# Where the attention scores stand in the instruction order of an audio-tower kernel

## The chip, the cores and the metric

The kernel runs on one core of one Trainium2 chip. The metric is device time in microseconds (us) of one execution. Three runs of the kernel before gave 1310.27, 1310.64 and 1313.44 us; the median is 1310.64. Everything is float32.

## The reference

For 64 sequences of 157 tokens with 512 features each, the reference does four things. `h` below is one sequence.

```python
frames = pad(x).reshape(64, 157, 512)
h = frames @ dct.T                                   # tokenizer
n = layernorm(h)
key = exp(1j * pi * tanh(n @ Wk + bk))               # 4 sets of 8 phases
qry = exp(1j * pi * tanh(n @ Wq + bq))
V = n @ Wv + bv
total = sum over sets and planes of weight * Re(cumsum(key * V) * conj(qry))
total = gate * total + (1 - gate) * pos_contrib      # gate = sigmoid(n @ Wg + bg)
h = h + n + total / norm @ Wo + bo
n = layernorm(h)
e = argmax(softmax(mean(n, axis=tokens) @ Wg_ffn + bg_ffn))   # one of 16 experts per sequence
h = h + gate_e * (n @ We[e] + be[e])
```

The cumulative sum over tokens is computed as a causally masked score matrix (key against query phases) times V. Each sequence picks one expert, whose 512x512 weights are gathered from memory.

## The kernel before, in words

The batch is cut into 16 groups `g` of four sequences (GB = 4). The 160 padded tokens are five blocks of 32 (Q = 32), so that one tile of 128 rows holds block `n` of all four sequences, 32 rows each. Block number 4 is called TAIL.

The program text writes each engine's order by hand: an instruction is issued on its engine where it stands in the text, and engines meet only at semaphores. For a middle group the order is: `project_and_values(g)`, `gate(g)`, `experts_and_embedding(g)`, `attention(g)`. The stages of three groups are interleaved. While group `g` computes gate and attention, the experts of group `g-1` run and the tokens of group `g+1` are embedded.

`gate(g)` computes the gate by seven block products (a fast matrix product scheme), in the order 1, 6, 2, 7, 5, 4, 3. Each product is four matmuls (`gate_product`, line 655), which the chip runs as eight passes. Products 2, 4 and 3 accumulate onto the PSUM bank of an earlier one (1, 7 and 5), after VectorE has read that bank. Between the products stand the five embeddings of group `g+1` (`embed`, lines 270 and 272; `embed_statistics`, in which ScalarE copies two pieces out of PSUM, lines 292 and 293, and VectorE reads the rest, lines 100 and 99, then takes mean and variance). Block 0 is embedded after product 6, block 1 after product 2, and blocks 2, 3 and TAIL after product 3. After product 5 stand `scores(g)` and `fold_twice(g+1, 1)`.

`scores(g)` computes the key-query products. For each of the five blocks and each of the four sequences it issues one matmul (line 681), 20 in all, with 128x32 weights; the output goes to the 32 rows of its sequence and uses columns 0 to 479 (NS = 480) of a 512-column bank. Then VectorE masks the result (line 682) and adds the position share (line 683) into `att`, which `read` in `attention(g)` uses.

`experts_and_embedding(g)` runs three of the five expert tiles of group `g-1`: TAIL, 0 and 1. An expert tile (`expert`, `expert_chunk`, line 945) is 16 matmuls of 128x32 weights and 512 columns, which the chip runs as 32 passes. Four of them, one per sequence, sit side by side in the array's columns. The stationary operand is `x2T`, the turned and normalised activations, moved by 16 small DMAs; the moving operand is `we`, the expert weights, one gathered megabyte per sequence (`fetch`, line 899, an indirect DMA on the GpSimd queue). Tiles 2 and 3 of the experts follow inside `attention(g)`.

PSUM is one pool of four buffers of two banks each (`psum`, and `bank` for its first bank). A request takes the next buffer, and its first write waits until the last reader of the buffer's former content is done.

Of the kernel before, what the change touches and what calls it, by code (L numbers as in the profile page):

```python
# [25 lines left out]
GB = 4  # L26
NG = B // GB
LP = 160
Q = P // GB
# [18 lines left out]
NS = sum(hi - lo for lo, hi in SEES)  # L48
# [5 lines left out]
def audio_tower(ctx: ExitStack, tc: tile.TileContext, a, out):  # L54
# [21 lines left out]
    nc = tc.nc  # L76
# [14 lines left out]
    def psum():  # L91

        return ps_mm.tile([P, 2, 512], F32, tag="mm", name="mm")

    def bank():
        return psum()[:, 0, :]

    S = [{} for _ in range(NG)]
# [10 lines left out]
    def load_half(g, m):  # L109

        if g < NG:
            if m == 0:
                S[g]["xT"] = p1.tile([P, C, 2 * HN], F32, tag="xT", name="xT", bufs=2)
            nc.sync.dma_start(out=half(S[g]["xT"], m), in_=a["frames"][g, m])

    def fold_once(g, m, engine=nc.gpsimd):

        if g < NG:
            ft = half(S[g]["xT"], m)
            even = p2.tile([P, 2, HN], F32, tag="even", name="even")  # L120
            add(even, ft[:, :2], ft[:, 2:])
            engine.tensor_tensor(ft[:, :2], ft[:, :2], ft[:, 2:], ALU.subtract)
            S[g]["even", m] = even

    def fold_twice(g, m):

        if g < NG:
            ft, even = half(S[g]["xT"], m), S[g].pop(("even", m))
            add(ft[:, 2], even[:, 0], even[:, 1])
            sub(ft[:, 3], even[:, 0], even[:, 1])  # L130
            for n in range(2):
                to, by = ft[:, n], ft[:, 1 - n]
                nc.vector.scalar_tensor_tensor(to, by, lift[:, n : n + 1], to, ALU.mult, ALU.add)
# [101 lines left out]
    def deviation(rstd, var):  # L235

        nc.gpsimd.tensor_scalar(rstd, var, EPS, None, ALU.add)  # L237
        nc.gpsimd.tensor_tensor(rstd, rstd, power[:, : rstd.shape[-1]], ALU.pow)

    def shifts(mean, rstd):  # L240

        shift = small.tile([P, NM], F32, tag="shift", name="shift")[:, : rstd.shape[-1]]
        nc.gpsimd.tensor_tensor(shift, mean, rstd, ALU.mult)
        nc.gpsimd.tensor_scalar(shift, shift, -1.0, None, ALU.mult)  # L244
        return shift
# [13 lines left out]
    def embed(g, n):  # L259

        s = S[g]
        if n == 0:
            s["res"] = {}
            s["res2"] = []
        h = psum()
        h, odd = h[:, 0, :], h[:, 1, :].rearrange("p (n j) -> p n j", n=2)
        by_r = h.rearrange("p (j r) -> p r j", r=4)
        ft = tile_of(s["xT"], n)
        for i in range(2):
            nc.tensor.matmul(by_r[:, 2 * i, :], ft[:, 2 + i], dct_e[:, i, :], start=True, stop=True)  # L270
        for i in range(2):
            nc.tensor.matmul(odd[:, i, : P + 1], ft[:, i], trig_o[:, i, :], start=True, stop=True)  # L272
        s["h", n] = h, odd
# [30 lines left out]
    def embed_deviations(g, of=range(NM), known=False):  # L304

        s = S[g]
        lo, hi = min(SLOT[n] for n in of), max(SLOT[n] for n in of) + 1
        rstd, mv = deviations[g % 2][:, lo:hi], s["mv"][:, lo:hi]
        if not known:
            deviation(rstd, mv[:, :, 1])  # L310
        shift = shifts(mv[:, :, 0], rstd)
        more = small.tile([P, NM], F32, tag="more", name="more", bufs=6)[:, : hi - lo]
        nc.gpsimd.tensor_scalar(more, rstd, 1.0, None, ALU.add)  # L313
        for n in of:
            k = slice(SLOT[n] - lo, SLOT[n] - lo + 1)
            s["rstd", n] = rstd[:, k]
            s["st", n] = shift[:, k], more[:, k]
# [194 lines left out]
    def add_bv(g, m, of=slice(0, D)):  # L512
        v = S[g]["v2", m][:, :, of]
        by = bv[:, of].unsqueeze(1).to_broadcast([P, 2, of.stop - of.start])
        nc.gpsimd.tensor_tensor(v, v, by, ALU.add)  # L515
# [131 lines left out]
    def gate_product(g, i):  # L647

        s = S[g]
        if i == 1:  # L650
            s["gT"] = p1.tile([P, C, 2 * HN], F32, tag="gT", name="gT")
        (ps, first), rhs, w = room(g, i), operand(g, i), fac_g[i]
        for o in range(2):
            for c in range(2):
                nc.tensor.matmul(  # L655
                    ps[:, o, :HN],
                    w[:, c, o * P : (o + 1) * P],
                    rhs[:, c],
                    start=(first and c == 0),
                    stop=(c == 1),  # L660
                    skip_group_check=not first,
                )
        part = halves(s["gT"])
        if i != 2:
            gather(i, by_halves(ps), part)
        for k, m, n in ((2, 0, 0), (5, 1, 1), (3, 0, 1), (4, 1, 0)):
            if k == i:
                for o in range(2):
                    to = part[m][n][:, o]
                    c = 2 * n + o  # L670
                    of = ps[:, o, :HN] if i == 2 else to
                    nc.scalar.activation(to, of, AF.Tanh, bias=hbg[:, c : c + 1], scale=0.5)  # L672

    def scores(g):

        ps = bank()
        for n in range(NM):
            lo, hi = SEES[n]
            for i in range(GB):
                to = ps[Q * i : Q * (i + 1), START[n] : START[n] + hi - lo]  # L680
                nc.tensor.matmul(to, kf[:, SLOT[n], i], qf[:, lo // Q : hi // Q, i], start=True, stop=True)  # L681
        nc.vector.tensor_tensor(att[:, 0], ps[:, :NS], hmask, ALU.mult)
        nc.vector.tensor_tensor(att[:, 1], att[:, 0], share, ALU.add)
# [223 lines left out]
    def pick_gate(g):  # L907

        s = S[g]
        logit, top, rev = (s.pop(k) for k in ("logit", "top", "rev"))  # L910
        nc.vector.tensor_tensor(logit, logit, over(top), ALU.subtract)
        nc.scalar.activation(logit, logit, AF.Exp)
        expf = t("expf", [P, 1])
        for i in range(GB):
            q = slice(Q * i, Q * (i + 1))
            nc.vector.tensor_scalar(expf[q], rev[q, i : i + 1], -1.0, float(E), ALU.mult, ALU.add)
        s["expi"] = expi = t("expi", [P, 1], I32)
        nc.vector.tensor_copy(expi, expf)
        den = t("den", [P, 1])
        for i in range(GB):  # L920
            q = slice(Q * i, Q * (i + 1))
            nc.vector.tensor_reduce(den[q], logit[q, i], AX.X, ALU.add)
        s["gate"] = gate = t("gate", [P, 1])
        nc.vector.reciprocal(gate, den)

    def bias(g):
        s = S[g]
        s["be"] = be = p2.tile([P, D], F32, tag="be", name="be", bufs=1)
        nc.gpsimd.indirect_dma_start(
            out=be,  # L930
            out_offset=None,
            in_=a["be"],
            in_offset=bass.IndirectOffsetOnAxis(ap=s["expi"], axis=0),
        )

    def add_bias(g, n):

        s = S[g]
        nc.vector.scalar_tensor_tensor(s["res"][n], s["be"], s["gate"], s["res"][n], ALU.mult, ALU.add)
# [25 lines left out]
    def expert(g, n, between=lambda c: None):  # L965
        ps = psum()
        for c in range(C):
            between(c)
            expert_chunk(g, n, c, ps[:, 0, :])
        between(C)  # L970
        expert_out(g, n, ps[:, 0, :])
# [166 lines left out]
    def gate(g):  # L1138
        ahead = g + 1 < NG
        for i in (1, 6, 2, 7, 5, 4, 3):  # L1140
            gate_product(g, i)
            if i == 1:
                pick_gate(g - 1)
                bias(g - 1)
                fold_once(g + 1, 1)
                add_bv(g, 0, slice(H, D))
                add_bv(g, 1)
            if i == 5:
                scores(g)
                fold_twice(g + 1, 1)  # L1150
            for n in {6: (0,), 2: (1,), 3: (2, 3, TAIL)}.get(i, ()) if ahead else ():
                embed(g + 1, n)
                embed_statistics(g + 1, n)

    def experts_and_embedding(g):

        new = g + 1
        embed_deviations(new)
        add_bias(g - 1, TAIL)
        add_bias(g - 1, 0)  # L1160
        expert(g - 1, TAIL)
        load_half(g + 2, 0)
        load_half(g + 2, 1)
        for n in (1, 2, 3):
            add_bias(g - 1, n)
        for n in range(NM):
            embed_res(new, n)
        expert(g - 1, 0)
        keep_deviations(new)
        expert(g - 1, 1)  # L1170
        spread_deviations(new)
# [69 lines left out]
    g = NG - 1  # L1241
# [158 lines left out]
```

## Time and profile before

| | |
|---|---|
| median of three runs | 1310.64 us |
| the profiled execution | 1311.08 us |
| its span, first to last instruction | 1309.1 us |
| granted TensorE clock | 0.999 |
| TensorE (PE) busy | 1302.9 us, 100% |
| weight loads (PEld) busy | 863.6 us, 66% |
| VectorE (DVE) busy | 1026.9 us, 78% |
| ScalarE (ACT) busy | 432.5 us, 33% |
| GpSimd (POOL) busy | 603.1 us, 46% |
| score matmuls, line 681 | 640 passes, 192 to 299 ns each |
| expert matmuls, line 945 with `we` | 2400 passes, 264.1 us busy, 593 ns each |
| memory traffic | 144.45 MB, mean 110 GB/s |

Times in the profile are microseconds from the start of the span. A busy time counts an engine as occupied while any of its instructions runs. A row of the timeline gives start, length, engine, source line, operation, `output<-inputs`, shape and count. For a matmul, `128*32 128x512` means weights of 128 rows and 32 columns and an output of 512 columns. Each float32 matmul of the program shows as two passes, so 20 score matmuls are 40 entries. In brackets at the end stands the idle time before a row and what ended it.

### The profile page before, as it was taken

How to read it: one execution, taken by the hardware profiler on the slowest of the kernel's cores; microseconds unless marked ns; L12 is line 12 of the kernel's file. 1: busy time of each engine (PE TensorE's matmuls, PEld its weight loads, DVE VectorE, ACT ScalarE, POOL GpSimd, SP SyncE). 2: the span in 40 equal slices, each digit the busy share in tenths (PEclk: the TensorE clock that was granted, in tenths of full speed). 3: DMA queues.
4: the chain of work that ended last, by engine and by line, in shares of the span. 5: the costliest groups of instructions: out<-in, count | busy, mean ns of one | idle time of the engine just before them, and what ended most of it. 6: DMA issues, size and time to landing. Idle time of an engine off the chain costs nothing.

```text
span 1309.1 us, 25859 instructions
## 1 busy us (share of the span) xinstructions
PE 1302.9 (100%) x10040; PEld 863.6 (66%) x10040; DVE 1026.9 (78%) x2056; ACT 432.5 (33%) x768; POOL 603.1 (46%) x766
## 2 busy tenths in 40 slices
PE   9999999999999999999999999999999999999998
PEld 6677666676666667666676666766666676666762
DVE  5888787788878878788787877888778787877673
ACT  2524334142432324334143331424323243341410
POOL 2356445344553446435364453446434364343424
PEclk9999999999999999999999999999999999999999
DMA  7015224152341425324252241523314252241506
GB/s 240 1 52 177 75 61 184 41 177 75 111 151 34 168 79 169 95 57 147 82 178 75 68 179 38 178 75 123 135 45 161 82 178 83 57 151 37 179 9 209
DMA packets 60578, 144.45 MB, mean 110 GB/s; under 512 B 14136, under 2 KB 31432, under 8 KB 52520
## 3 DMA queue, kind: packets, MB, share of 16 engines
q1 hardware_dynamic: 45620, 62.68, 16.9%
q0 software_dynamic: 14336, 79.47, 16.7%
q8 instruction: 80, 1.31, 0.4%
q10 hardware_dynamic: 500, 0.64, 0.2%
q14 instruction: 42, 0.34, 0.1%
HBM read 102.47 MB, written 20.62 MB: 94 GB/s over the span
## 4 chain that ended last, share of the span: by engine, by line
PE 98%; POOL 1%; DMA 1%; issue 0%; DVE 0%; POOLq 0%
PE mm L445 29%; PE mm L945 20%; PE mm L655 18%; PE mm L250 9%; PE mm L697 9%; PE mm L270 3%; PE mm L272 3%; PE mm L600 3%; PE mm L636 1%; PE mm L681 1%; PE mm L201 1%; DMA t_v<-in_we,rows 1%; PE mm L219 0%; PE mm L191 0%; PE mm L840 0%
## 5 line engine op out<-in xcount | busy, mean ns | idle before, releaser
L945 PE MATMUL mm<-we,x2T 128*32 128x512 f32 x2400 | 264.1, 593 | 0.0
L945 PEld LDWEIGHTS mm<-we,x2T 128*32 128x32 f32 x2400 | 74.8, 110 | 167.3 <-issue 165.5
L237 POOL TENSOR_SCALAR rstd<-mv 128x2 f32<-128x2 f32 (+1 forms) x50 | 11.8, 236 | 292.6 <-DVE mv L233 292.5
L697 PE MATMUL mm<-att,v 32*128 32x320 f32 (+3 forms) x2048 | 113.1, 357 | 0.0
L697 PEld LDWEIGHTS mm<-att,v 32*128 32x128 f32 x2048 | 94.5, 185 | 22.1 <-issue 12.6
L956 DVE SCALAR_TENSOR_TENSOR res<-mm,gate,res 128x512 f32<-128x512 f32 x64 | 47.9, 749 | 73.1 <-PE mm L945 73.1
L237 POOL TENSOR_SCALAR dev<-mv 128x5 f32<-128x5 f32 (+1 forms) x20 | 10.5, 525 | 196.8 <-DVE mv L233 196.2
L776 ACT ACTIVATE x<-res,shift,rstd 128x512 f32<-128x512 f32 x61 | 46.4, 806 | 162.6 <-POOL shift L244 161.4
L704 DVE TENSOR_TENSOR gT<-mm,gT 128x320 f32<-128x320 f32 x128 | 59.5, 484 | 42.6 <-PE mm L697 42.5
L100 DVE TENSOR_TENSOR gT<-mm,gT 128x320 f32<-128x320 f32 (+3 forms) x128 | 71.4, 567 | 23.9 <-PE mm L655 20.9
L232 DVE BATCH_NORM_STATS2 st<-res 128x6 f32<-128x512 f32 x128 | 87.7, 685 | 2.8
L327 POOL TENSOR_TENSOR res<-res,bo 128x512 f32<-128x512 f32 x64 | 81.6, 1288 | 13.1 <-ACT res L323 13.0
L445 PE MATMUL mm<-t_o,sum 128*128 128x256 f32 x384 | 85.5, 379 | 0.0
L515 POOL TENSOR_TENSOR v<-v,bv 128x512 f32<-128x512 f32 (+1 forms) x45 | 72.7, 1635 | 24.5 <-ACT v L464 24.4
L672 ACT ACTIVATE gT<-gT,hbg 128x320 f32<-128x320 f32 x90 | 45.6, 554 | 112.8 <-DVE gT L100 112.8
L323 ACT ACTIVATE res<-res,shift,more 128x512 f32<-128x512 f32 x64 | 46.9, 803 | 103.7 <-POOL more L313 103.7
L445 PE MATMUL mm<-t_v,sum 128*128 128x256 f32 x360 | 80.1, 379 | 0.0
L445 PEld LDWEIGHTS mm<-t_o,sum 128*128 128x128 f32 x384 | 73.0, 190 | 9.9
L899 POOL DMA_INDIRECT we<-in_we,rows x60 | 60.4, 1006 | 34.3 <-DVE rows L895 20.3
L445 PEld LDWEIGHTS mm<-t_v,sum 128*128 128x128 f32 x360 | 68.4, 190 | 9.3
L250 PE MATMUL mm<-wv,xT 128*128 128x512 f32 x160 | 71.8, 592 | 0.0
L655 PE MATMUL mm<-xT,wg 128*128 128x320 f32 x240 | 69.5, 432 | 0.0
(220 smaller groups left out, 2877.9 us busy)
## 6 DMA issues: line engine op xcount, KB each, us to landing
xT<-in_frames SPq DMA_DIRECT2D x32, 640.0 KB
out<-res SPq DMA_DIRECT2D x236, 64.0 KB
x2T<-turned SPq DMA_DIRECT2D x150, 80.0 KB
x2T<-turned POOLq DMA_DIRECT2D x90, 80.0 KB
scale<-row SPq DMA_DIRECT2D x15, 320.0 KB
out<-res_t SPq DMA_DIRECT2D x62, 32.0 KB
out<-res_t SPq DMA_DIRECT2D x62, 26.0 KB
wg<-in_wg SPq DMA_DIRECT2D x1, 1024.0 KB
```

The lines of the kernel that those rows point to most:

```text
L100: add = lambda *x: nc.vector.tensor_tensor(*x, ALU.add)
L232: nc.vector.bn_stats(st, h)
L250: nc.tensor.matmul(ps, tile_of(x[:, c], n), w[:, c, :], start=(c == 0), stop=(c == C - 1))
L327: nc.gpsimd.tensor_tensor(r, r, bo, ALU.add)
L445: nc.tensor.matmul(ps[:, b, :], lhs[:, c, P * b : P * (b + 1)], w[:, c, :], start=(first and c == 0), stop=(c == 1), skip_group_check=not ...
L515: nc.gpsimd.tensor_tensor(v, v, by, ALU.add)
L655: nc.tensor.matmul(ps[:, o, :HN], w[:, c, o * P : (o + 1) * P], rhs[:, c], start=(first and c == 0), stop=(c == 1), skip_group_check=not f ...
L697: nc.tensor.matmul(to, s["v", n][q, c * P : (c + 1) * P], by, start=(n == 3), stop=(n == TAIL))
L704: nc.vector.tensor_tensor(th, r[:, :, 0], th, ALU.mult)
L899: nc.gpsimd.indirect_dma_start(out=ws[b][:, n * k : n * (k + 1)], out_offset=None, in_=of, in_offset=bass.IndirectOffsetOnAxis(ap=rows[:, ...
L945: nc.tensor.matmul(ps[Q * i : Q * (i + 1), :], s["x2T"][:, c, i, Q * n : Q * (n + 1)], s["ws"][i][:, c, :], start=(c == 0), stop=(c == C - 1),
L956: nc.vector.scalar_tensor_tensor(o, ps, s["gate"], o, ALU.mult, ALU.add)
```

## The change

`scores(g)` gets a second way to be called. With `met=g-1` it first issues four short matmuls, one per sequence. Each takes 32 columns of that sequence's `x2T` as weights and 32 columns of its expert weights as the moving operand, and writes 32 columns into the unused end (columns 480 to 511) of the score bank. Nobody reads that output. Then the 20 score matmuls follow as before.

For groups 1 to 14 the call leaves `gate(g)` and stands at the head of `experts_and_embedding(g)`, ahead of everything else in it, so that on TensorE the order is: gate products 5, 4 and 3, the last three embeddings, the four short matmuls, the scores, the first expert tile. VectorE's two score operations move with it, behind the statistics of the last three embeddings. Groups 0 (`first_gate`) and 15 (the last, not `ahead`) keep their scores where they were.

```diff
-    def scores(g):
+    def scores(g, met=None):
 
         ps = bank()
+        for i in range(GB) if met is not None else ():
+            x, w = S[met]["x2T"], S[met]["ws"][i]
+            to = ps[Q * i : Q * (i + 1), NS : NS + Q]
+            nc.tensor.matmul(to, x[:, 0, i, :Q], w[:, 0, :Q], start=True, stop=True)
         for n in range(NM):
             lo, hi = SEES[n]
             for i in range(GB):
...
             if i == 5:
-                scores(g)
+                if not ahead:
+                    scores(g)
                 fold_twice(g + 1, 1)
...
     def experts_and_embedding(g):
 
         new = g + 1
+        scores(g, met=g - 1)
         embed_deviations(new)
         add_bias(g - 1, TAIL)
```

## The prediction

> **What bounds the kernel now.** I read the page's totals first, then the chain that ended last, then who waited for whom on TensorE.
>
> ```profile
> span 1309.1 us, 25859 instructions
> PE 1302.9 (100%) x10040; PEld 863.6 (66%) x10040; DVE 1026.9 (78%) x2056; ACT 432.5 (33%) x768; POOL 603.1 (46%) x766
> ...
> PE 98%; POOL 1%; DMA 1%; issue 0%; DVE 0%; POOLq 0%
> ```
>
> TensorE is busy for the whole span and is 98% of the last chain. The waits view puts only 1.6 us of idle on PE in all, none of it at the scores or at the 14 first expert tiles. So there is no wait for this change to remove: only the number and spacing of TensorE instructions can move the time. Durations cannot show the spacing, because a 128x512 matmul lasts 593 ns in the table while its neighbour starts earlier. Start times can. The timeline of PE for one group (g = 2), and then for the seam between experts and projection in the group before:
>
> ```profile
> 200.65 2.32 PE L655 MATMUL mm<-sum,wg 128*128 128x320 f32 x8
> 202.80 2.32 PE L655 MATMUL mm<-sum,t_g 128*128 128x320 f32 x8
> 205.05 1.03 PE L681 MATMUL mm<-qf,kf 128*32 128x128 f32 x40
> 206.01 2.42 PE L655 MATMUL mm<-xT,t_g 128*128 128x320 f32 x8
> 208.27 2.32 PE L655 MATMUL mm<-sum,wg 128*128 128x320 f32 x8
> 210.43 0.61 PE L270 MATMUL mm<-dct_e,xT 128*128 128x128 f32 x4
> ```
>
> ```profile
> 167.21 7.08 PE L945 MATMUL mm<-we,x2T 128*32 128x512 f32 x64
> 174.10 2.34 PE L600 MATMUL mm<-xT,wkq 128*32 128x320 f32 x32
> 176.37 1.99 PE L445 MATMUL mm<-wv,xT 128*128 128x256 f32 x8
> 178.20 0.59 PE L250 MATMUL mm<-wv,xT 128*128 128x512 f32 x1
> ```
>
> Columns are start, length, line, operation, weights (rows*columns), shape, count. Eight gate matmuls (L655) take 202.80 - 200.65 = 2.15 us, 0.269 each. From 202.80 to 210.43 there are 24 of them and the scores: 7.63 - 24 x 0.269 = 1.17 us for the scores. With starts read to the nanosecond it is 1.162 or 1.163 us in each of the 14 groups.
>
> Part of that is the seam. Gate matmuls use 128*128 weights; scores, like experts, use 128*32. Entering: 205.05 - 202.80 - 2.15 = 0.10 (0.094 to the nanosecond), and the first score pass takes 0.133 where its twin takes 0.109, another 0.024. Leaving: 206.01 comes 0.118 late, and 206.01 to 208.27 is 2.26, again 0.10 over 2.15. Sum 0.34 us; the scores' own streaming is 1.163 - 0.340 = 0.823. The second fence confirms both halves. L945 to L600 (both 128*32) pays nothing: 16 steps of 0.429 plus the 0.024 at entry make 6.89, just 174.10 - 167.21. L600 to L445 pays: 2.27 for eight steps of 0.269, then 1.83 for eight of 0.216, so 0.12 + 0.10.
>
> **What the Trainium skill says.** "TensorEngine Tiling (Array Packing)", section Tiling Modes, Key Properties: "Changing tiling mode (not just tile) drains the TensorE". The trace agrees, with 0.12 us in and 0.22 us out, and nothing between two users of one mode. "TensorE: Matmul & The Clock Gate", section Wait — 56ns, not 53.3ns?, gives a floor of about 25 ns start to start per small matmul. This trace has 6 to 7 ns between the four column tiles of a step, and 28 ns for a whole four-wide step of width 32; the measurement decides. "Trace Analysis", section Per-instruction lifecycle, says that TensorE's end times are a model: hence starts only.
>
> **The change, part by part.** It applies to g = 1 to 14, 14 groups; g = 0 and g = 15 keep their scores in place.
>
> *Removed from the gate:* 1.163 us per group, since then the eight matmuls at 206.01 follow their predecessor after 0.269, as those at 208.27 do. They wait for the DVE pair at 203.49 that reads the bank they add onto. It ends at 204.35 and their weights would load at 204.69, so 0.3 us is left. The next eight need the pair of 205.16, done at 206.06, against 207.11. Covered; if that cover failed, the first would be late by what it lacks.
>
> *Added at the head of the expert tile:* the same 20 score matmuls, 0.823 us, plus four of width 32. Each is two passes, so two four-wide steps. The trace has exactly this step in the last score block: starts at 205.840 and 205.868, 0.028 apart; so 0.056. With the skill's floor on all eight passes it would be 0.20; the trace's own shape is preferred, and no gain is possible from added matmuls. Entry to the narrow mode was already paid there by the first expert matmul (213.20 after the last embedding matmul at 212.99: 0.20 where 0.11 is usual, then 0.024); the four short ones now pay it. After the scores no seam, as from L945 to L600.
>
> Per group: -1.163 + 0.823 + 0.056 = -0.284 us. Times 14: -3.98 us.
>
> *The weight waits.* The short matmuls take over the waits on x2T and the four weight gathers, 1.16 us earlier. The windows just before the first expert matmul of groups 2 and 4 show that this costs nothing (last two columns: DMA share, GB/s):
>
> ```profile
> 209.80:213.00 3.20, 3.20 (x27) 2.96 (x26) 1.18 (x3) 2.53 (x7) 0.00 (x0) 1.00 0.00 0
> 368.50:371.70 3.20, 3.20 (x27) 2.96 (x26) 1.18 (x3) 2.53 (x7) 0.00 (x0) 1.00 0.02 5
> ```
>
> In all 14 groups the DMA share there is 0.00 to 0.03 (the 0.03 is a stray bias row). The data has been there for over 3 us. The nine wait instructions of 51 ns (about 0.11 apart) that the sequencer spends run while the embedding matmuls stream, as now.
>
> *DVE.* Two operations of 0.66 us (L682, L683) leave the gate and land behind the three embeddings' statistics, ahead of the bias adds. The embedding's DVE work moves 1.16 earlier with its matmuls and 1.32 is inserted: the first expert bank is read 0.16 us later. Reading of V, which needs `att`, starts at 223.6, and DVE idles 1.26 us before the last expert read. Hidden. ACT, POOL, SP and the DMAs get nothing new; the load issued behind the first expert tile's output is some 0.2 us later, tens of us ahead of its reader.
>
> *Banks.* Here is the one new risk. Four PSUM buffers go round, in the order of asking. Before, the first expert tile took the bank of the last gate product; now the scores take that one, and the tile takes the bank of embedding 2, one embedding more recent. Its last reader is DVE's L99:
>
> ```profile
> 211.49 1.01 ACT L672 ACTIVATE gT<-gT,hbg 128x320 f32<-128x320 f32 x2 [0.28 <-DVE gT L100]
> 212.41 0.25 ACT L292 COPY sines<-mm 128x129 f32<-128x129 f32 x1
> 212.55 0.61 ACT L293 COPY res<-mm 128x256 f32<-128x256 f32 x1
> ```
>
> ```profile
> 210.62 0.82 DVE L100 TENSOR_TENSOR gT<-mm,gT 128x640 f32<-128x640 f32 x1 [0.47 <-PE mm L655]
> 213.20 0.41 DVE L100 TENSOR_TENSOR res<-mm,sines 128x128 f32<-128x128 f32 x1 [1.75 <-ACT res L293]
> 213.44 0.42 DVE L99 TENSOR_TENSOR res<-mm,sines 128x128 f32<-128x128 f32 x1
> ```
>
> This chain hangs on the last gate product (0.47 and 1.75 us of idle waiting for PE and ACT), so it moves with PE: its end, 213.87, becomes 213.87 - 1.16 = 212.70. The expert tile wants to start at 213.196 - 1.163 + 0.056 + 0.024 + 0.823 = 212.94. Elsewhere in this trace a wait instruction starts 0.03 after its update, takes 0.051, and its load follows 0.025 later: 212.81. The tile's four matmuls then arrive 0.036 apart (as after the blocked wait at 75.35), the fourth at 212.92 for a start near 212.96. Cover: 0.13 us for the first, some 0.04 for the fourth. Each 0.1 us beyond it costs 1.4 us in the whole.
>
> **The sum.** The profiled execution took 1311.08 us, its span 1309.1, with 2 us around it; the span becomes 1305.1. The median shown is 0.44 below that execution. The saving carries over unchanged: 1310.64 - 3.98 = 1306.66, a ratio of 0.9970. A measurement of this kernel can tell about 0.3% (3.93 us) from no change, so the forecast stands right on that bound.
>
> **Rivals.**
> *The bank takes back part.* The tile's wait on embedding 2 falls short by 0.05 to 0.2 us: 0.7 to 2.8 us of 3.98 are lost, 1307.4 to 1309.5. For it: the cover of 0.04 to 0.13 is the thinnest anywhere. Against: every link was followed and moves with PE. 17 in 100.
>
> *Slower: embedding 2's bank is not freed earlier.* If the ACT and DVE work stays where it is, the tile cannot start before 213.87 + 0.11 = 213.98, 1.04 after its slot: -0.284 + 1.04 = +0.76 per group, 1321 us. It turns the sign when the chain moves by less than about 0.74 of the 1.16 us, and passes 0.3% when it moves by less than 0.46. Against: DVE's idle of 1.75 us says that it was waiting, not late. 6 in 100, half-way cases from 1311 included.
>
> *Slower: weights late.* The scores now stand behind the gathers. This decides only when a gather lands 2 us later than in any of the 14 windows; each us beyond is 14 us, so 1320 and more. 2 in 100.
>
> *The seam does not vanish, or more does.* If leaving the gate's matmuls unbroken saves only the entry (0.118), net 0.06 a group: 1309.8; 3 in 100. If releasing DVE in the gate also removes small delays that I see no wait for: 1304 to 1305.5; 4 in 100.
>
> **How the numbers follow.** The forecast itself has 68 in 100, spread between 1306.0 and 1307.4, so the bound cuts it. Its seam costs repeat to 1 ns in 14 groups, its centre is just past the bound, and the sum counts no gain from the freed DVE: 0.56 faster and 0.12 within. Adding the larger gain: faster 0.60. Within 0.3%: 0.12 + 0.17 + 0.03 = 0.32. Slower: 0.08. The range 1305.7 to 1308.8 holds the forecast and most of the partial loss, and leaves out the two slow cases, the largest gain and the worst of the rest.
>
> **What would show it.** In the changed profile: the gate's L655 rows 2.15 us apart with no 2.26 among them; a PE row of the four short matmuls and the scores ahead of the expert tile, about 0.90 us from its start to the first expert matmul; the groups' period 0.28 us shorter. A wait of the expert tile for DVE `res`, or that distance at 1.0 or more, is the bank; a wait for DMA at the short matmuls is the weights. I am wrong if the distance is right and the span is not 4 us shorter.

## The result and the profile after

The changed kernel takes 1307.14 us, median of eight runs (1306.21 to 1309.04), against 1310.79 us for the kernel before in the same comparison (1310.12 to 1313.44). The ratio is 0.997 with a 95% interval of 0.9961 to 0.998: 3.65 us faster, right at the size that can be told from no change. A second measurement of the same two kernels gave 1307.57 against 1311.07 us, 0.9977 (0.9966 to 0.9989).

The page of the kernel after, its totals and the chain that ended last:

```profile
span 1306.9 us, 26083 instructions
PE 1300.8 (100%) x10152; PEld 864.4 (66%) x10152; DVE 1038.8 (79%) x2056; ACT 432.1 (33%) x768; POOL 601.5 (46%) x766
...
PE 98%; POOL 1%; DMA 1%; issue 0%; DVE 0%; POOLq 0%
```

TensorE has 112 passes more (10152 against 10040: eight in each of 14 groups) and is still the whole chain. This execution's span is only 2.2 us shorter than the one shown of before, 1309.1. That misleads because of the start of the kernel, which is shown further down. First, one group. The timeline of PE, g = 2 (the line numbers have moved: scores 685, short matmuls 680, experts 949):

```profile
202.40 2.32 PE L655 MATMUL mm<-sum,wg 128*128 128x320 f32 x8
204.56 2.32 PE L655 MATMUL mm<-sum,t_g 128*128 128x320 f32 x8
206.71 2.32 PE L655 MATMUL mm<-xT,t_g 128*128 128x320 f32 x8
208.86 2.32 PE L655 MATMUL mm<-sum,wg 128*128 128x320 f32 x8
211.01 0.61 PE L270 MATMUL mm<-dct_e,xT 128*128 128x128 f32 x4
...
213.25 0.61 PE L272 MATMUL mm<-trig_o,xT 128*128 128x129 f32 x4
213.79 0.27 PE L680 MATMUL mm<-we,x2T 128*32 128x32 f32 x8
213.87 1.01 PE L685 MATMUL mm<-qf,kf 128*32 128x128 f32 x40
214.70 0.62 PE L949 MATMUL mm<-we,x2T 128*32 128x512 f32 x4
```

The four gate rows stand 2.15 to 2.16 us apart: the row of 0.96 for the scores and the 2.26 behind it are gone. The short matmuls cost 213.87 - 213.79 = 0.08 us from start to start, of which 0.024 is the slower first step after the change of weight shape (the rest of that change stands ahead of them, where it stood before); the scores cost 214.70 - 213.87 = 0.83 us; together 0.91 us (0.914 read to the nanosecond) from the first short matmul to the expert tile. There is no bracket at the end of the tile's row, so the trace names no idle time ahead of it.

The length of the repeated part is read best from one line's first and last start. Line 600 is the projection, 32 passes in each of 16 groups; the two numbers after the durations are the start of the first pass (group 0) and of the last (group 15), so their difference covers all 14 changed groups, and neither the start of the kernel nor its end. Before, then after:

```profile
L600 PE MATMUL mm<-xT,wkq x512: 432/432/457, 45.8 to 1207.6; 128*32 128x320 f32 x171
```

```profile
L600 PE MATMUL mm<-xT,wkq x512: 432/432/457, 47.8 to 1205.7; 128*32 128x320 f32 x171
```

Before, 1207.6 - 45.8 = 1161.8 us; after, 1205.7 - 47.8 = 1157.9 us: 3.9 us less, 0.28 in each group. With starts read to the nanosecond the period between the projections of groups 1 and 15 fell from 79.345 to 79.064 us, by 0.281. But the first projection began 2.0 us later in this execution. That comes from the start of the kernel, which the change does not touch. The start, in the timeline of PE, before and then after:

```profile
4.93 2.05 PE L201 MATMUL mm<-wkq,tables 128*128 128x64 f32 x12
6.82 5.37 PE L201 MATMUL mm<-wv,tables 128*128 128x512 f32 x12
12.03 4.43 PE L219 MATMUL mm<-total,tables 128*128 128x512 f32 x16
```

```profile
4.93 2.66 PE L201 MATMUL mm<-wkq,tables 128*128 128x64 f32 x12
7.38 6.85 PE L201 MATMUL mm<-wv,tables 128*128 128x512 f32 x12
14.06 4.43 PE L219 MATMUL mm<-total,tables 128*128 128x512 f32 x16
```

Same instructions, 2.03 us more between 4.93 and the row of line 219. Over the ten profiled executions of this study the first projection starts between 45.6 and 48.0 us with no order by kernel: a second execution of the changed kernel had 46.6, and a version of the kernel before had 48.0. This alone spreads totals by up to 2.4 us, against an effect of 3.9. So the experiments below are read in two ways: the timed median, and the distance from first to last projection of the profiled execution, which does not contain the start.

| experiment and kernel | median us | ratio to before (95%) | first to last projection, us | difference from before |
|---|---|---|---|---|
| before | 1310.79 | | 1161.87 | |
| after | 1307.14 | 0.997 (0.9961 to 0.998) | 1157.94 | -3.93 |
| 1: after, again | 1307.57 | 0.9977 (0.9966 to 0.9989) | 1158.02 | -3.85 |
| 2: scores behind the first tile, no short matmuls | 1307.8 | 0.997 (0.9958 to 0.9982) | 1157.41 | -4.47 |
| 3: before, scores behind product 3 | 1310.88 | 0.9999 (0.999 to 1.0008) | 1161.72 | -0.15 |
| 4: before, scores cut in two | 1315.81 | 1.0035 (1.0023 to 1.0048) | 1166.49 | +4.62 |
| 5: before with the short matmuls | 1311.84 | 1.0006 (1.0 to 1.0013) | 1162.60 | +0.72 |
| 6: after without the short matmuls | 1316.89 | 1.0047 (1.0032 to 1.0063) | 1167.61 | +5.73 |
| 7: after, bank read late | 1318.24 | 1.0055 (1.0039 to 1.0072) | 1169.05 | +7.17 |
| 8: before, bank read late | 1313.14 | 1.0017 (1.001 to 1.0023) | 1163.76 | +1.88 |

The distances are read to the nanosecond. The kernel before was timed anew beside the experiments: 1311.07 us beside 1, 2, 5 and 6, and 1311.13 us beside 3, 4, 7 and 8; the ratios are to those.

### The profile page after: what moved, and what is told of

It reads as the page before. It is cut to its first block, busy times and chain, and to the rows that moved or that the text cites. A ratio compares the mean times of both kernels' runs of the same rounds, so it can differ in the third digit from the quotient of the medians.

```text
span 1306.9 us, 26083 instructions
## 1 busy us (share of the span) xinstructions
PE 1300.8 (100%) x10152; PEld 864.4 (66%) x10152; DVE 1038.8 (79%) x2056; ACT 432.1 (33%) x768; POOL 601.5 (46%) x766
## 4 chain that ended last, share of the span: by engine, by line
PE 98%; POOL 1%; DMA 1%; issue 0%; DVE 0%; POOLq 0%
PE mm L445 29%; PE mm L949 20%; PE mm L655 17%; PE mm L250 9%; PE mm L701 9%; PE mm L270 3%; PE mm L272 3%; PE mm L600 3%; PE mm L636 1%; PE mm L201 1%; PE mm L685 1%; DMA t_v<-in_we,rows 1%; PE mm L219 0%; PE mm L191 0%; PE mm L680 0%
## 5 line engine op out<-in xcount | busy, mean ns | idle before, releaser
L327 POOL TENSOR_TENSOR res<-res,bo 128x512 f32<-128x512 f32 x64 | 96.3, 1517 | 13.1 <-ACT res L323 13.0
L237 POOL TENSOR_SCALAR dev<-mv 128x5 f32<-128x5 f32 (+1 forms) x20 | 4.9, 244 | 182.0 <-DVE mv L233 181.4
L672 ACT ACTIVATE gT<-gT,hbg 128x320 f32<-128x320 f32 x90 | 45.6, 554 | 100.7 <-DVE gT L100 100.7
L712 POOL TENSOR_TENSOR gT<-gT,rest 128x320 f32<-128x320 f32 x60 | 50.6, 865 | 43.0 <-ACT rest L711 42.9
```

Source lines behind the costliest of these rows:

```text
L327: nc.gpsimd.tensor_tensor(r, r, bo, ALU.add)
L712: nc.gpsimd.tensor_tensor(th, th, rest, ALU.add)
```

## The experiments

**The theories.** *Seam*: the time comes from the changes between 128*128 and 128*32 weights that the scores made inside the gate. *Freed gate*: it comes from VectorE and the gate's accumulating products, which no longer have the scores' two operations between them. For the two new things, the short matmuls and the bank, the question is what they cost and whether they were needed.

**1. The changed kernel once more,** with no edit beyond the change.

> The changed kernel once more, beside the others of this batch. Both theories: 3.6 to 4.0 us below the kernel before, the first expert tile starting 0.90 to 0.92 us behind the short matmuls, one group every 79.08 us.

It measured 1307.57 us, 3.5 below its kernel before, just short of the 3.6 expected, and 3.85 us in the distance of the projections. The gain repeats.

**2. The scores behind the first expert tile, without the short matmuls.** This has no change of weight shape at either end, and it leaves the tile's bank as before.

```diff
             if i == 5:
-                scores(g)
+                if not ahead:
+                    scores(g)
...
         expert(g - 1, TAIL)
+        scores(g)
```

> The scores stand behind the first expert tile instead of ahead of it, and there are no short matmuls: the tile's own first four matmuls take the waits on weights and activations as before. Seam theory (the gain is the two mode changes around the scores, 0.34 us a group): the seam is gone here too and the 0.056 us of short matmuls are saved, so one group every 79.02 us and 4.4 to 4.8 us below the kernel before, some 0.8 us below the changed kernel. Freed-gate theory (the gain comes from taking the scores and their VectorE work out of the gate): the same as the changed kernel, 3.6 to 4.0 us below before.

Its timeline of PE around the scores, g = 2:

```profile
214.04 3.64 PE L945 MATMUL mm<-we,x2T 128*32 128x512 f32 x32
217.49 1.01 PE L681 MATMUL mm<-qf,kf 128*32 128x128 f32 x40
218.32 7.05 PE L945 MATMUL mm<-we,x2T 128*32 128x512 f32 x64
```

The scores take 218.32 - 217.49 = 0.83 us between two users of the same weight shape, which is the 0.823 us that the prediction had derived as their own streaming. In the gate they took 1.163. The medians (1307.8 here, 1307.57 for the changed kernel) do not tell the two versions apart: this one is 3.3 us below before, where seam expected 4.4 to 4.8 and freed gate 3.6 to 4.0. The periods, from one execution each, do: 0.320 us less per group than before, against 0.281 and 0.275 in the two executions of the changed kernel. The gap of about 0.04 us is near the price of the short matmuls, as seam predicts. Whether this version is faster in the whole, by some 0.5 us, is not shown, and between the two theories it is experiment 3 that decides.

**3. The scores behind product 3.** Out of the middle of the gate, but still between two users of 128*128 weights. VectorE and the accumulating products are freed; the seam stays.

```diff
             if i == 5:
-                scores(g)
+                if not ahead:
+                    scores(g)
...
+            if i == 3 and ahead:
+                scores(g)
```

> The kernel before with the scores moved from behind product 5 to behind product 3, still between two pieces of wide work (product 3 and embedding 2), in 14 groups; no short matmuls. The stretch between products 5 and 4 is freed as in the changed kernel, but the two mode changes stay. Seam theory: no change, within 0.5 us of the kernel before. Freed-gate theory: 3 to 4 us below it.

1310.88 us, ratio 0.9999: no change. The timeline of PE shows the seam in its new place:

```profile
206.08 2.32 PE L655 MATMUL mm<-xT,t_g 128*128 128x320 f32 x8
208.23 2.32 PE L655 MATMUL mm<-sum,wg 128*128 128x320 f32 x8
210.48 1.03 PE L681 MATMUL mm<-qf,kf 128*32 128x128 f32 x40
211.44 0.71 PE L270 MATMUL mm<-dct_e,xT 128*128 128x128 f32 x4
211.99 0.61 PE L272 MATMUL mm<-trig_o,xT 128*128 128x129 f32 x4
```

The gate's rows are 2.15 apart here too. But the scores come 210.48 - 208.23 - 2.15 = 0.10 late, they take 0.96 instead of 0.83 to the next row, and the first embedding row takes 0.55 where the others take 0.45. The same costs stand in another place, and the gain is gone. Freed gate falls: with VectorE's two operations out of the gate and the seam kept, the period changes by 0.011 us.

**4. The scores cut in two.** Blocks 0, 1 and 2 stay behind product 5; blocks 3 and TAIL with the VectorE work go behind product 4. One seam more, no other work. (The lines that let `scores` take a part of the blocks are left out.)

```diff
...
             if i == 5:
-                scores(g)
+                part = scores(g, (0, 1, 2))
                 fold_twice(g + 1, 1)
+            if i == 4:
+                scores(g, (3, TAIL), part)
```

> The kernel before with the scores cut in two: twelve matmuls after product 5, the other eight and the VectorE work after product 4, in the same bank. Same matmuls, one more pair of mode changes in 15 groups. Seam theory: 0.34 us more in each, 5.1 us above the kernel before, each L655 set behind a part starting 0.12 late and losing 0.10 more. Freed-gate theory: nothing, or a little faster, since VectorE's score work comes later in the gate.

1315.81 us, 4.7 above before, where 5.1 had been expected; in the period +0.330 us, where one seam had been put at 0.340. Its timeline of PE has both:

```profile
202.96 2.32 PE L655 MATMUL mm<-sum,t_g 128*128 128x320 f32 x8
205.21 0.70 PE L681 MATMUL mm<-qf,kf 128*32 128x128 f32 x24
205.84 2.42 PE L655 MATMUL mm<-xT,t_g 128*128 128x320 f32 x8
208.19 0.54 PE L681 MATMUL mm<-qf,kf 128*32 128x160 f32 x16
208.66 2.42 PE L655 MATMUL mm<-sum,wg 128*128 128x320 f32 x8
210.92 0.61 PE L270 MATMUL mm<-dct_e,xT 128*128 128x128 f32 x4
```

Two gate rows now have length 2.42 and reach 2.35 and 2.26 us to the next row. Adding a seam costs about what removing one gains (0.330 against the 0.340 worked out for the gate), so the price goes with the change of shape and not with the place.

**5. The short matmuls alone,** in the kernel before, ahead of its first expert tile and into the tile's own bank.

```diff
-    def expert(g, n, between=lambda c: None):
+    def expert(g, n, between=lambda c: None, met=False):
         ps = psum()
+        for i in range(GB) if met else ():
+            x, w = S[g]["x2T"], S[g]["ws"][i]
+            nc.tensor.matmul(ps[Q * i : Q * (i + 1), 0, :Q], x[:, 0, i, :Q], w[:, 0, :Q], start=True, stop=True)
...
-        expert(g - 1, TAIL)
+        expert(g - 1, TAIL, met=True)
```

> The kernel before with only the four short matmuls added, ahead of the first expert tile and into that tile's own bank; the scores stay in the gate. Both theories: two steps of 0.028 us a group, 14 groups, 0.8 us above the kernel before. If a short matmul has a floor of 25 ns a pass: 0.2 us a group, 2.8 us above.

1311.84 us, 0.77 above before, and +0.051 us in the period; 14 x 0.051 = 0.7. By themselves they are a small cost and bring nothing; the 0.2 us a group of the floor that the prediction quotes is excluded.

**6. The changed kernel without the short matmuls.**

```diff
         new = g + 1
-        scores(g, met=g - 1)
+        scores(g)
```

> The changed kernel without its four short matmuls: the scores are moved, and the wait instructions for weights and activations stand between the last score and the first expert matmul. Seam theory: the nine or so wait instructions, 0.11 us each, are reached with only about eight matmuls of work queued (0.4 us), so the four matmuls of the first expert step start one by one and the last is 0.5 to 0.8 us late; against the kernel before -0.34 + 0.65 = +0.3 us a group, 2 to 7 us above it. If the short matmuls serve nothing: 0.056 us a group better than the changed kernel, 4.4 to 4.8 us below before.

1316.89 us, 5.8 above the kernel before and 9.3 above the changed one. The page's waits do not say why: on PE they have the one at the start and 0.4 us for a DMA in the last group. The timeline of PE does, g = 2:

```profile
212.68 1.03 PE L685 MATMUL mm<-qf,kf 128*32 128x128 f32 x40
213.60 11.16 PE L949 MATMUL mm<-we,x2T 128*32 128x512 f32 x96
224.69 1.80 PE L701 MATMUL mm<-att,v 32*128 32x320 f32 x32
```

From the first expert pass to the reading of V are 224.69 - 213.60 = 11.09 us, for three tiles that take 225.12 - 214.70 = 10.42 us in the changed kernel. And the first of them starts 0.92 us after the scores instead of 0.83. The sum, 0.76, less the 0.08 that the short matmuls took from start to start, agrees with the 0.69 us by which this kernel's period is longer (79.754 against 79.064). What differs is where TensorE's sequencer, which issues its instructions, meets the nine wait instructions for `x2T` and the gathered weights. One line's entries within g = 2, in this kernel and then in the changed one (op, count, durations, first and last start):

```profile
L949 PEldq EVENT_SEMAPHORE  x12: 51/51/51, 213.1 to 217.9; - x12
```

```profile
L680 PEldq EVENT_SEMAPHORE  x9: 51/51/51, 211.7 to 212.7; - x9
```

In the changed kernel the nine are over by 212.7, one us before the short matmuls start at 213.79: they run while the embeddings stream. The tile's own wait, for its bank, follows alone at 214.49. Without the short matmuls all ten stand behind the scores and run from 213.14 to 214.19, 0.11 to 0.14 us apart (two of the twelve counted belong to the later tiles). In the changed kernel the sequencer meets the first of them with 17 passes still to start ahead of their user, and here with 20. But 17 embedding passes take 2.1 us, and 20 score passes only 0.46.

Four of the ten stand ahead of the weights of the tile's first column and two ahead of those of each other column: the loads of the four columns, taken in the order of the program, start at 213.57, 213.80, 214.03 and 214.26. The first eight weight loads of the tile (four columns, two passes each), in this kernel and then in the changed one:

```profile
213.57 0.84 PEld L949 LDWEIGHTS mm<-we,x2T 128*32 128x32 f32 x8
```

```profile
214.67 0.17 PEld L949 LDWEIGHTS mm<-we,x2T 128*32 128x32 f32 x8
```

So the four columns start one by one, at 0, 232, 464 and 695 ns, where the changed kernel has 0, 7, 13 and 20. The passes of one column still follow each other every 0.43 us, and nothing brings the columns together again: through all three tiles the starts of a step are 35, 197, 35 and 161 ns apart, instead of three times 7 and then 409. The fourth column, 0.67 us late at the start, is 0.67 us late at the end (its last pass starts 10.57 us after the tile's first, against 9.89), and the reading of V follows 0.52 us after that last pass in both kernels. So the short matmuls pay 0.05 us to have the waits met where something hides them. The data is not what is late: the ten waits follow each other evenly, no idle time of PE for a DMA shows outside the last group, and in g = 2 the bank was released at 213.34, before the wait for it began at 213.39.

**7. The changed kernel with embedding 2's bank read late.** ScalarE's copy of `sines` is made four times for that block in each of the 14 changed groups, so the bank that the first expert tile takes comes free later.

```diff
-        nc.scalar.copy(sines, odd[:, 1, : P + 1])
+        for _ in range(4 if n == 2 and 1 < g < NG else 1):
+            nc.scalar.copy(sines, odd[:, 1, : P + 1])
```

> The changed kernel, with ScalarE's first copy of embedding 2 made four times over instead of once, so that the bank which the first expert tile takes is freed 0.4 to 0.6 us later. Bank reading: the tile's cover of some 0.13 us is used up and the rest shows as a wait, 0.3 to 0.45 us a group, 4 to 6.5 us above the changed kernel, that is 0 to 2.5 us above the kernel before; the tile starts 1.2 to 1.4 us behind the short matmuls instead of 0.91. If the bank has more cover than I worked out: no change against the changed kernel.

1318.24 us, 10.7 above the changed kernel as measured in 1, where 4 to 6.5 had been expected. The waits of PE, and the timeline of PE in g = 2:

```profile
PE mm L950 <- DVE res L99: 8.3, 14, 0.6
```

```profile
212.78 0.27 PE L681 MATMUL mm<-we,x2T 128*32 128x32 f32 x8
212.87 1.01 PE L686 MATMUL mm<-qf,kf 128*32 128x128 f32 x40
214.47 10.51 PE L950 MATMUL mm<-we,x2T 128*32 128x512 f32 x96 [0.59 <-DVE res L99]
```

Fourteen waits, one in each group, on the operation that the prediction had named. The tile starts 1.60 us after the scores instead of 0.83. It starts 1.891 us after the start of the last embedding matmul, against 1.117 in the changed kernel: 0.775 us of stall, 14 x 0.775 = 10.9 us. (The bracket and the view of waits count only from the shown end of the last score matmul, hence 0.59 and 8.3.) The size was off because each added copy took 0.30 us and not the 0.14 to 0.2 that the expectation implies: the bank's release moved from 0.873 to 1.756 us after the last embedding matmul, by 0.88.

This gives the bank's cover in the changed kernel, that is, how much later it could be released before the tile waits; no wait shows it there. From the release to the tile's first matmul the blocked case needs 1.891 - 1.756 = 0.135 us. Unblocked, 1.117 - 0.873 = 0.244 us are there. So 0.244 - 0.135 = 0.11 us were left. (These are means over the 14 groups, with the release read from VectorE's semaphore.) The changed kernel's timeline of DVE shows the two operations ahead of that release:

```profile
213.79 0.41 DVE L100 TENSOR_TENSOR res<-mm,sines 128x128 f32<-128x128 f32 x1 [1.75 <-ACT res L293]
214.03 0.42 DVE L99 TENSOR_TENSOR res<-mm,sines 128x128 f32<-128x128 f32 x1
```

The second ends its use of the bank at 214.46 and the tile starts at 214.70. VectorE idles 1.75 us for ScalarE ahead of them, as before, and ends 0.87 us after the last embedding matmul starts (0.86 before): the chain moved with TensorE.

**8. The same late read in the kernel before,** as a control; its first expert tile takes another bank.

> The control to the run before it: the same three extra copies in the kernel before, where the second expert tile takes that bank, 3.4 us later. Both readings: no change, within 0.5 us of the kernel before.

This missed: 1313.14 us, 2.0 above before, and the period 0.134 us longer. The first expert tile is not the cause: it starts 0.20 us after the last embedding matmul, as ever. The time goes some 15 us later, in the fourth reading of V, whose second half waits for ScalarE to empty a bank. ScalarE's timeline there, one row of the kernel before and then the control's:

```profile
221.87 2.94 ACT L323 ACTIVATE res<-res,shift,more 128x512 f32<-128x512 f32 x4 [7.08 <-POOL more L313]
```

```profile
225.21 2.93 ACT L324 ACTIVATE res<-res,shift,more 128x512 f32<-128x512 f32 x4 [7.10 <-POOL more L314]
...
230.36 0.43 ACT L708 COPY rest<-mm 128x320 f32<-128x320 f32 x1 [0.88 <-DVE gT L705]
230.95 0.43 ACT L708 COPY rest<-mm 128x320 f32<-128x320 f32 x1 [0.17 <-POOL gT L709]
```

The late copy delays the embeddings' statistics, these delay GpSimd's part (`more`), and ScalarE starts its normalising block at 225.21, 0.8 us before the reading of V begins on TensorE (226.03). In the kernel before it starts at 221.87, 1.8 us before (223.63). Its copies for the reading come late in turn. The fourth reading lasts 233.31 - 231.31 = 2.00 us, against 230.76 - 228.91 = 1.85 before. So in the kernel before this chain seems to have had less than the 0.9 us of cover by which it was made late. This is read from the rows of the two traces; no further run isolates it. In the changed kernel the embeddings end 0.90 us earlier against the reading (their last matmul starts 11.53 us ahead of it, against 10.63), and its run with the same late copy shows no such loss: the 10.9 us of its bank wait account for nearly all of its 11.1 us in the distance of the projections.

## Why the prediction was right

**The time.** 1306.7 us was predicted, 1307.14 and 1307.57 were measured, within the range. The sum of 0.284 us per group and 3.98 us in all met 0.281 and 0.275 us per group and 3.93 and 3.85 us. That the median moved by 3.65 and 3.5 and not by 3.9 lies within what the start scatters. The mark that would have proved the sum wrong, "the distance is right and the span is not 4 us shorter", turned out to be badly chosen: the distance is right, the one profiled span is 2.2 us shorter, and the start, ahead of the first changed group, took 2.0 us more. The period was the right mark and the span was not. The forecast put the saving right at the 0.3% that a measurement can tell from no change and gave the far side of it the larger chance; the medians fell just on the near side (0.28% and 0.27%). With a start that scatters by 2 us, which side it is was chance.

**Removed from the gate, 1.163 us.** Confirmed: all gate rows are 2.15 to 2.16 apart. Its two parts were confirmed apart from each other: 0.823 of streaming by experiment 2, where it was 0.83, and 0.340 of seam by experiment 4, which measured 0.330. The Trainium skill's sentence in "TensorEngine Tiling (Array Packing)", section Tiling Modes, Key Properties, that changing the mode drains TensorE, fits what was timed here: each change between 128*128 and 128*32 weights lost time, and nothing was lost between two users of 128*32. The amounts, 0.12 us in and 0.22 us out, are this trace's; no run shows the drain itself.

**Added at the tile, 0.823 + 0.056.** Confirmed, with a small miss: a step of width 32 took 0.032 us instead of 0.028 where a wider one follows it, which happens twice, and the first score step took 0.112 instead of 0.109, so that the distance from short matmuls to expert tile was 0.914 and not 0.904. Experiment 5 has their cost in the whole at 0.051 per group. The 0.20 us, an estimate with the Trainium skill's floor of about 25 ns per matmul ("TensorE: Matmul & The Clock Gate", section Wait — 56ns, not 53.3ns?) on all eight passes, is excluded. The prediction costed the short matmuls, but treated the wait instructions as hidden "as now", and did not say that the scores alone would uncover them. Experiment 6 shows that this part carries 0.69 us per group: without it the change would have lost 5.8 us.

**Weights and DVE.** No wait of the short matmuls for a DMA appears, and no idle time of PE in the gate or at the tile. No experiment made the weights late. The VectorE work stayed hidden, but with less to spare than the prediction's 0.16 us suggests. In g = 2 the first expert bank is read 0.11 us later, counted from the gate; yet the 1.26 us that VectorE idled ahead of the last expert read are gone in all 14 groups, mostly because one bias add there takes 1.77 us instead of 0.74. GpSimd's addition (L327) that runs at the same time in g = 2 takes 1.88 us instead of 1.29. No run shows the cause. In experiment 2 no bias add is stretched.

**The bank.** The mechanism, the bank taken and the operation that frees it were right, and experiment 7 turns the wait on. The sizes: 0.11 us of cover was there and 0.13 predicted. The step between release and start was 0.135 us, and 0.106 (0.03 + 0.051 + 0.025), which ends at the weight load, had been added up. The thinner cover of 0.04 for the fourth matmul did not appear: behind the blocked wait the four start 7 ns apart. The rate "each 0.1 us beyond costs 1.4 us" holds: 0.775 us of stall in each group cost 10.9.

**The rivals.** The bank did not take back a part, though it needed only 0.11 us to begin. Embedding 2's chain did move with TensorE. The seam vanished wholly (the gate rows of the profile after; experiment 4 for its size). The larger gain from a freed VectorE did not come, and experiment 3 shows that there was none.

## What to carry to other kernels

On a TensorE that is always busy, read starts, not durations: count the places where the weights' shape changes, price one from a neighbouring row, and put users of one shape side by side. A block that moves takes its place in the buffer rotation and its wait instructions with it. So look up who now takes whose buffer and how long before it is wanted it comes free, and where in the queue the waits stand: in experiment 6 waits that were already satisfied still cost 0.69 us a group, because only short matmuls ran ahead of them, and TensorE's view of waits does not list it. When the effect is of the size of the start's scatter, compare the period inside the loop.

## What the runs showed that was not expected

- A staggered start lasts. In experiment 6 ten wait instructions of 51 ns each, met 0.11 to 0.14 us apart, put the array's four columns out of step, and they stayed so for 11 us, through three tiles, with the same 0.43 us from pass to pass of each column. The cost of 0.67 us is the lateness of the fourth column, which the next stage waited for.
- A copy repeated into the same tile was dearer than expected. In experiment 7 the fourfold copy of 128x129 moved the bank's release by 0.88 us, near 0.30 us for each added one: each repeat started 0.03 us after the end of the one before it. In the changed kernel the next piece starts 0.15 us after the start of the single copy, 0.10 us before that copy's end.
- A delay of 0.9 us on ScalarE in the embeddings came out some 15 us later as 0.13 us a group on TensorE (experiment 8; the path is read from the trace, not isolated), although ScalarE is busy for 33% of the span only.
